# Reordering the opening, adj's squares and layer 1's last pair in a four-layer graph kernel bound by TensorE

## The chip, the cores and the metric

The kernel runs on one core of one Trainium2 chip. The metric is the device time of one execution in microseconds (us); smaller is better. Every experiment was timed on the same chip as the kernel before, in alternating rounds. All runs told of here were fast runs; their granted clock was 0.998 to 1.0 of full. A run takes about 970 us, so 1 us is 0.1%; differences under about 0.5 us are at the edge of what the timings can tell.

## The reference, cut to what matters

`x` has the shape 32 x 512 x 128 and `adj` 512 x 512, both float32. Each of four layers adds its output to `x`; each takes `h = relu(layernorm(x))` as input.

```python
# layer 0: masked softmax attention, one row of weights for all batches
m   = adj > 0
idx = jnp.cumsum(m.reshape(-1).astype(jnp.int32)) - 1
A   = softmax(where(m, e[0][idx], NEG), axis=1)
out = einsum('ij,bjg->big', A * I, h @ W[0]) + einsum('ij,bjg->big', A * (1 - I), h @ W[1]) + bias
# layer 1: Chebyshev hops with adj, then Theta and relu
x1 = einsum('bnf,nw->bwf', h, adj);  x2 = 2.0 * einsum('bnf,nw->bwf', x1, adj) - h
out = relu(concat(h, x1, x2, x1, x2) @ Theta + bias)
# layer 2: messages with adj * adj
features = relu(h @ psi_w + psi_b)
messages = einsum('nm,bnd->bmd', adj * adj, features)
out = relu(concat(messages, h) @ phi1_w + phi1_b) @ phi2_w + phi2_b
# layer 3: attention with tanh-clipped scores
A = exp(tanh(Q @ K.T / sqrt(128) / 8) * 8) * adj;  out = (A / A.sum(-1)) @ h @ v
```

## The kernel before: the parts that the change touches

The 32 batches are handled as 16 pairs (`NQ = 16`). The large products with adj use seven block products where eight would be plain (Strassen's scheme), so some operands are sums of blocks, made by VectorE (DVE) and GpSimd (POOL). Python generators interleave the work: each `yield` is a place where another stage's instructions may be put between. In the traces here each engine runs them in the order in which the program issues them (the products p_qk_t, p_later and p_qk, issued sooner, start at 8.6 to 9.8 us after the change and at 13.3 to 15.2 us before it). That order is what the change changes.

The opening finds, from `adj`, which value of `e` belongs to each entry, by products with 0/1 matrices; in the same time it normalises pair 0.

```python
    # adj > 0 and row counts rc, as adj lands; rch is their half-precision copy
    nc.vector.tensor_copy(rch, rc)
    # ... p_incl: cumulative counts, on TensorE
    keep_busy(7)                                   # dummy products p_idle
    early = [early_stats(q, q == 1) for q in range(2)]
    next(early[0])                                 # statistics of pair 0's first batch
    # ... known, incl, before
    go(normal[0], NT)                              # ScalarE normalises that batch
    for t in range(NT):                            # of_row on VectorE, p_row on TensorE
        # ...
    # ... p_known
    next(early[0])                                 # statistics of pair 0's second batch
    nc.tensor.transpose(p[:, blk(0)], qw, ident)   # layer 3's q and k
    nc.tensor.transpose(p[:, blk(1)], kw, ident)
    nc.scalar.copy(pgs[:, 0:2, :], pg[0])
    nc.vector.tensor_copy(pgs[:, 2:4, :], pg[1])
    # ... p_upto, which needs pgs
    nc.tensor.matmul(p_qk[:, :D], qkT[:, 0, :], qkT[:, 1, :], start=True, stop=True)
    for t in range(NT):                            # "mask products", p_later
        nc.tensor.matmul(scores[t], ident16, m[:, t, :], start=True, stop=False)
    go(normal[0])                                  # second batch of pair 0
    # ... p_hT: transposes of h; p_g: projections with W
```

adj transposed goes to memory by way of four VectorE transposes and four DMA writes; the same SyncE queue carries the feature-major copies hT of later pairs.

```python
    def turn_adj():
        for t in range(NT):
            nc.vector.transpose(ab[:, :, t, :], adj_s[:, t, :].rearrange(...))
            yield
        for b in range(NQR):
            nc.sync.dma_start(adjT_d[:, blk(b)]..., ab[b * QR : (b + 1) * QR]...)
    # in round 0 of layer 0:  step 3: go(squares, 2)   step 4: go(squares)
```

In layer 1 `first(C)` computes a hop, `weighed(C)` multiplies by Theta (32 products p_w), and `right_blocks` makes the sums that the second hop's products p_l need. Between them is a `yield`, which lets the next stage's products in; for the last pair, that is layer 2's.

```python
        weighed(A)
        first(C)
        yield
        def operands():
            weighed(C)
            return right_blocks(...)
        if r == 0:
            right2 = operands()
        yield
        if r > 0:
            right2 = operands()
        # ... the products p_l
        if C == NQ - 1:
            yield
            yield
            yield
        ln_stats(A)
        ln_stats(C)
```

## Time and profile before

| | kernel before |
|---|---|
| median of three runs | 971.31 us (971.03 to 971.39) |
| profiled span | 969.8 us |
| TensorE busy | 956.6 us, 99% |
| VectorE, ScalarE, GpSimd busy | 60%, 49%, 43% |
| mean granted TensorE clock | full |

TensorE (PE) leaves 13.2 us of its span unused, and the other engines are idle for about half of it. In such a kernel no other engine's total matters; only the single places do where PE stands and waits for one of them. The profile's lines for these places are in the prediction below. One caution on reading them: a matmul's end is modelled, so a PE that is slightly held up at every product looks busy. The distance between the starts of two products is the safer measure.

### The profile page before, as it was taken

Reading aid. Unit: us, or ns where it says so; the run is one execution under the profiler, and the core shown is the slowest. Engines: PE = TensorE matmul, PEld = TensorE weight load, DVE = VectorE, ACT = ScalarE, POOL = GpSimd, SP = SyncE. Lnnn points to the kernel's source line nnn. Section 1 sums busy time; section 2 is a strip of 40 time slices with the busy share of each in tenths; the row PEclk is TensorE's granted clock in tenths of the full one; section 3 lists DMA queues with packets and bytes.
Section 4 is the critical chain, followed back from the end, with each engine's and each line's share of the span. In section 5 each row is a group of like instructions: output and inputs, shape, how many; then the busy total and the mean of one; then the engine's idle time right before and its main releaser. Section 6 shows DMA issues by size and latency. Waiting matters only on the chain.

```text
span 969.8 us, 15164 instructions
## 1 busy us (share of the span) xinstructions
PE 956.6 (99%) x5473; PEld 780.9 (81%) x5473; DVE 584.6 (60%) x1332; ACT 471.1 (49%) x1055; POOL 421.1 (43%) x463
## 2 busy tenths in 40 slices
PE   8999999999999999999999999999999999999998
PEld 4889999898998989897887777777676777777776
DVE  7788986745546536646657756655654444454444
ACT  4864551452242233376628544455674445544553
POOL 4867997933417523512324443334042233223322
PEclk9999999999999999999999999999999999999999
DMA  9075643242341321343343332332131121121111
GB/s 247 21 195 163 175 109 99 74 123 66 95 139 33 82 70 40 109 109 88 72 125 108 110 87 66 87 88 73 57 100 56 49 73 54 57 74 45 55 33 44
DMA packets 83913, 86.04 MB, mean 89 GB/s; under 512 B 6784, under 2 KB 74624, under 8 KB 83840
## 3 DMA queue, kind: packets, MB, share of 16 engines
q1 hardware_dynamic: 83840, 85.09, 31.3%
q8 instruction: 43, 0.70, 0.3%
q14 instruction: 30, 0.25, 0.1%
HBM read 44.17 MB, written 40.89 MB: 88 GB/s over the span
## 4 chain that ended last, share of the span: by engine, by line
PE 90%; DVE 3%; POOL 2%; ACT 2%; DMA 1%; issue 1%; SPq 0%; DVEq 0%; POOLq 0%; ACTq 0%
PE p_av L1112 12%; PE p_score L1097 11%; PE p_l_c L382 7%; PE p_w L431 5%; PE p_l_d L382 5%; PE p_msgT_c L375 5%; PE p_x1T_c L375 4%; PE p_l_a L382 4%; PE p_hv L431 3%; PE p_l L431 3%; PE p_qkh L1084 3%; PE p_msgT_d L375 3%; PE p_feat L431 3%; PE p_phi L1067 3%; PE p_phi L1068 3%; PE p_msgT_a L375 3%
## 5 line engine op out<-in xcount | busy, mean ns | idle before, releaser
L243 ACT ACTIVATE h<-x,sh,rs 128x128 f32<-128x128 f32 x512 | 209.4, 484 | 65.6 <-PE p_x1T_d L375 21.6
L1102 POOL TENSOR_TENSOR ex<-ex,adjTx 128x512 f32<-128x512 f32 x62 | 80.4, 1297 | 208.2 <-ACT ex L1100 202.6
L1098 ACT ACTIVATE ex<-p_score 128x512 f32<-128x512 f32 x128 | 71.8, 587 | 122.9 <-issue 113.1
L1112 PEld LDWEIGHTS p_av<-qkh_hv,ex 128*128 128x128 f32 x1024 | 118.4, 191 | 8.4 <-issue 7.4
L1112 PE MATMUL p_av<-qkh_hv,ex 128*128 128x129 f32 x1024 | 119.9, 274 | 0.0
L1097 PE MATMUL p_score<-qkh_hv,hT 128*128 128x512 f32 x256 | 115.2, 593 | 0.0
L1102 DVE TENSOR_TENSOR ex<-ex,adjTx 128x512 f32<-128x512 f32 x66 | 46.1, 702 | 81.9 <-ACT ex L1100 81.9
L279 DVE STREAM_TRANSPOSE hb_hT<-h 128x512 f32<-128x512 f32 x120 | 81.9, 697 | 20.9 <-ACT h L243 19.2
L223 DVE BATCH_NORM_STATS2 bn<-x 128x6 f32<-128x256 f32 x248 | 89.8, 417 | 0.6
L1097 PEld LDWEIGHTS p_score<-qkh_hv,hT 128*128 128x128 f32 x256 | 46.2, 190 | 46.5 <-issue 44.7
L1100 ACT ACTIVATE ex<-ex 128x512 f32<-128x512 f32 x128 | 76.6, 630 | 1.8
L352 POOL TENSOR_TENSOR rt_feat<-feat,feat 128x256 f32<-128x256 f32 x16 | 11.6, 725 | 140.1 <-ACT feat L1051 140.1
L949 ACT COPY w<-p_w 128x512 f32<-128x512 f32 x32 | 18.2, 574 | 106.2 <-PE p_w L431 106.1
L352 POOL TENSOR_TENSOR rt_w<-w,rt_w 128x512 f32<-128x512 f32 x16 | 20.3, 1270 | 110.3 <-DVE rt_w L352 92.0
L431 PE MATMUL p_w<-th,x1T 128*128 128x128 f32 x256 | 49.5, 275 | 0.0
L431 PE MATMUL p_w<-th,hs 128*128 128x128 f32 x256 | 49.5, 275 | 0.0
L431 PEld LDWEIGHTS p_hv<-vw,hT 128*128 128x128 f32 x256 | 33.6, 192 | 15.3 <-issue 8.1
L1062 POOL TENSOR_TENSOR x<-x,phi2b 128x256 f32<-128x256 f32 x64 | 44.5, 726 | 0.0
L431 PEld LDWEIGHTS p_w<-th,hs 128*128 128x128 f32 x256 | 39.9, 192 | 0.7
L1117 DVE SCALAR_TENSOR_TENSOR x<-p_av,rsum,x 128x128 f32<-128x128 f32 x128 | 39.1, 347 | 1.9
L1051 ACT ACTIVATE feat<-feat 128x512 f32<-128x512 f32 x32 | 20.1, 629 | 40.9 <-DVE feat L1050 40.9
L700 POOL TENSOR_TENSOR hd<-hT,adiag 128x512 f32<-128x512 f32 x32 | 39.7, 1276 | 0.3 <-ACT adiag L827 0.3
(234 smaller groups left out, 2040.2 us busy)
## 6 DMA issues: line engine op xcount, KB each, us to landing
d_hT<-hb_hT SPq DMA_DIRECT2D x240, 128.0 KB
hT<-d_hT SPq DMA_DIRECT2D x60, 512.0 KB
x<-in_x_dram SPq DMA_DIRECT2D x32, 256.0 KB
out_dram<-x SPq DMA_DIRECT2D x31, 256.0 KB
adj_s<-in_adj_dram SPq DMA_DIRECT2D x4, 256.0 KB
adjT_d<-adj_squares SPq DMA_DIRECT2D x4, 256.0 KB
sq<-in_adj_dram SPq DMA_DIRECT2D x4, 256.0 KB
adjTx<-adjT_d SPq DMA_DIRECT2D x4, 256.0 KB
```

Of the source, the lines that this page charges most:

```text
L223: nc.vector.bn_stats(st[:, k].rearrange("p e s -> p (e s)"), xt[q][:, b, t : t + 2, :].rearrange("p t f -> p f t"))
L243: nc.scalar.activation(h[:, b, t, :], xt[q][:, b, t, :], AF.Relu, bias=shift[q][:, i : i + 1], scale=scale[q][:, i : i + 1])
L279: nc.vector.transpose(hb[:, :, b].rearrange("p j t r -> p t j r"), h[:, b].rearrange("p t (j c) -> p t j c", c=QR))
L375: nc.tensor.matmul(p[:, :H], b[:, k, :], a[:, k, :], start=(first and k == 0), stop=(k == 1), skip_group_check=True)
L382: nc.tensor.matmul(p[:, i * 2 * D : (i + 1) * 2 * D], a[:, k, blk(i)], b[:, k], start=(first and i == 0 and k == 0), stop=(k == 1), skip_g ...
L431: nc.tensor.matmul(p[:, blk(t)], hT(t), w, start=(i == 0), stop=(i == len(terms) - 1))
L1062: tc.keep_in_program_order(nc.gpsimd.tensor_add(xi, xi, spread(phi2b, 2)))
L1097: nc.tensor.matmul(ps, hT[:, t, b, :], qkh, start=True, stop=True)
L1098: nc.scalar.activation(ex[:, t, :], ps, AF.Tanh, scale=1.0 / (8.0 * math.sqrt(D)))
L1100: nc.scalar.activation(ex[:, t, :], ex[:, t, :], AF.Exp, scale=8.0)
L1102: eng.tensor_mul(split(ex[:, t, :]), split(ex[:, t, :]), crossed(adjTx[0][:, t, :]))
L1112: nc.tensor.matmul(po[:, i, : D + 1], ex[:, t, blk(i0 + i)], hv[:, t, :], start=(t == 0), stop=(t == NT - 1))
```

## The change

The intent is to close PE's holes by order alone: no product is added and none dropped but four dummies. It has four parts.

```diff
# 1. the opening
     for b in range(2):
         load_x(b)
+    qw = load_rows(q_w, "qw")[:, 0, :]          # before: behind the next two x loads
+    kw = load_rows(k_w, "kw")[:, 0, :]
 ...
             if whole and b == 0:
+                yield                           # pair 1's statistics in two parts
                 continue
 ...
-    keep_busy(7)
+    # one of known's two copies moves ahead of adj's as well
+    # q/k transposes and qkT's copy, mask products p_later, p_qk and qk's copy: here now
+    keep_busy(3)
     early = [early_stats(q, q == 1) for q in range(2)]
     next(early[0])
 ...
+    next(early[0])                              # pair 0's second statistics before of_row
 ...
-    go(normal[0], NT)
+    go(normal[0])                               # all eight normalisations before pgs
 ...                                             # row products p_row, p_known
-    next(early[0])
-    # (q/k transposes, p_qk, p_later, go(normal[0]) stood behind here)
+    next(early[1])

# 2. adj's squares: created before the first softmax, then one step at a time
     go(early_stats_2, 3)
+    next(squares)
 ...
                     next(left_of_att)
+                    next(squares)
                     go(ln3)
 ...
-                    go(squares, 2)              # step 3 of round 0
+                    go(squares)
 ...
-                    go(squares)                 # step 4 of round 0
 ...                                             # rounds 2 and up: one product later
-                if more and r > 1:
-                    go(projection(A + 2))       # step 1
-                if r == 1:
+                if more:
                     go(projection(A + 2))       # step 2

# 3. layer 1's last pair weighed sooner
-        if r == 0:
+        sooner = r == 0 or C == NQ - 1
+        if sooner:
             right2 = operands()
         yield
-        if r > 0:
+        if not sooner:
             right2 = operands()

# 4. its statistics in two rounds
-        if C == NQ - 1:
-            yield
-            yield
-            yield
-        ln_stats(A)
-        ln_stats(C)
+        if C < NQ - 1:
+            ln_stats(A)
+            ln_stats(C)
+
+    def layer1_stats():
+        ln_stats(NQ - 2)
+        yield
+        ln_stats(NQ - 1)
 ...
+    waiting[-NQ + 7].append(layer1_stats())
```

More of the change, by code (lines that the diff above doesn't have):

```diff
@@ L142 @@
         load_x(b)
-    qw = load_rows(q_w, "qw")[:, 0, :]
-    kw = load_rows(k_w, "kw")[:, 0, :]
     w0 = const.tile([P, 2, D], F32, name="w0")
@@ L183 @@
     nc.vector.memset(ones, 1.0)
+    known = prep.tile([P, NT, 2], F16, name="known")
+    nc.vector.tensor_copy(known[:, :, 1], rows)
     upto = prep.tile([P, NT, N], F16, name="upto")
@@ L515 @@
                              start=(s == 0), stop=(s == t))
-    keep_busy(7)
+    p = bank("p_qk_t")
+    nc.tensor.transpose(p[:, blk(0)], qw, ident)
+    nc.tensor.transpose(p[:, blk(1)], kw, ident)
+    qkT = prep.tile([P, 2, D], F32, name="qkT")
+    nc.scalar.copy(qkT, tiles(p)[:, :2, :])
+    scores = {}
+    for t in range(NT):
+        scores[t] = bank(f"p_later_{t}")
+        nc.tensor.matmul(scores[t], ident16, m[:, t, :], start=True, stop=False)
+    p_qk = bank("p_qk")
+    nc.tensor.matmul(p_qk[:, :D], qkT[:, 0, :], qkT[:, 1, :], start=True, stop=True)
+    qk = const.tile([P, D], F32, name="qk")
+    nc.scalar.copy(qk, p_qk[:, :D])
+    keep_busy(3)
     early = [early_stats(q, q == 1) for q in range(2)]
     next(early[0])
-    known = prep.tile([P, NT, 2], F16, name="known")
-    nc.vector.tensor_copy(known[:, :, 1], rows)
     incl = prep.tile([P, NT], F32, name="incl")
@@ L561 @@
                              start=(t == 0), stop=(t == NT - 1))
-    next(early[0])
-    p = bank("p_qk_t")
-    nc.tensor.transpose(p[:, blk(0)], qw, ident)
-    nc.tensor.transpose(p[:, blk(1)], kw, ident)
-    qkT = prep.tile([P, 2, D], F32, name="qkT")
+    next(early[1])
     pgs = prep.tile([P, NT, NE], F16, name="pgs")
@@ L570 @@
     nc.vector.tensor_copy(pgs[:, 2:4, :], pg[1])
-    nc.scalar.copy(qkT, tiles(p)[:, :2, :])
     row_of = prep.tile([P, NK], F32, name="row_of")
@@ L581 @@
                              start=(j == 0), stop=(j == NT - 1), skip_group_check=True)
-    p_qk = bank("p_qk")
-    nc.tensor.matmul(p_qk[:, :D], qkT[:, 0, :], qkT[:, 1, :], start=True, stop=True)
-    qk = const.tile([P, D], F32, name="qk")
-    nc.scalar.copy(qk, p_qk[:, :D])
-    scores = {}
-    for t in range(NT):
-        scores[t] = bank(f"p_later_{t}")
-        nc.tensor.matmul(scores[t], ident16, m[:, t, :], start=True, stop=False)
-    go(normal[0])
     copies = [nc.scalar.copy, (nc.scalar.copy, nc.vector.tensor_copy), nc.scalar.copy]
@@ L650 @@
     attT = square_tile("attT")
+    squares = turn_adj()
     early_stats_2 = stats_steps(2)
@@ L721 @@
     own, turning, hd, adiag = {}, {}, {}, []
-    squares = turn_adj()
     sums_ahead = late_sums()
```

## The prediction

> **What bounds the kernel now.** I read the page first, then the waits of TensorE (PE), the timeline of every engine over the first 75 us, and the queue of SyncE (SP), which issues the transfers.
>
> ```profile
> span 969.8 us, 15164 instructions
> PE 956.6 (99%) x5473; PEld 780.9 (81%) x5473; DVE 584.6 (60%) x1332; ACT 471.1 (49%) x1055; POOL 421.1 (43%) x463
> PE 90%; DVE 3%; POOL 2%; ACT 2%; DMA 1%; issue 1%; SPq 0%; DVEq 0%; POOLq 0%; ACTq 0%
> ```
>
> PE is the bound: it is idle for 969.8 - 956.6 = 13.2 us, and the chain that ended last is PE for nine tenths. No matrix work leaves the kernel except four dummy products, so the change can win only PE's holes. The waits of PE name them (line, releaser, total, count, longest):
>
> ```profile
> PE p_g L431 <- DMA hT<-d_hT: 2.1, 2, 1.2
> PE p_idle L496 <- DVE upto L186: 1.9, 1, 1.9
> PE p_incl L514 <- DVE rch L509: 1.0, 1, 1.0
> PE p_msgT_a L375 <- ACT feat L1051: 0.9, 1, 0.9
> PE p_msgT_c L375 <- POOL rt_feat L352: 0.7, 1, 0.7
> PE p_l_a L382 <- ACT w L949: 0.7, 1, 0.7
> PE p_msgT_c L375 <- DVE msgT L398: 0.6, 1, 0.6
> PE p_msgT_a L375 <- ACT msgT L396: 0.5, 1, 0.5
> ```
>
> The two waits on hT are at 60.93 and 70.87 us, the feat, msgT copy and rt_feat waits between 452 and 457 us, the one on DVE msgT at 515.43 us, the one on w at 390.00 us. Short stalls hide inside busy time, so I also compared start-to-start times with the usual one of each shape (0.112 us for a 128x128 f32 product, 0.216 us for 128x256 f32 or 128x512 f16). By that the hT holes are 1.33 and 1.12 us, the 452-457 ones 1.07 + 0.68 + 0.89 = 2.64 us, and the 515 one 0.78 us and 0.21 us right after it.
>
> The opening is the other place. PE's timeline (start, us, product):
>
> ```profile
> 10.51 2.75 PE L555 MATMUL p_row<-of_row,m 128*128 128x256 f16 x16 [0.33 <-DVE of_row L552]
> ...
> 13.72 1.37 PE L580 MATMUL p_upto<-upto,pgs 128*128 128x512 f16 x8
> 14.93 0.44 PE L583 MATMUL p_qk<-qkT 128*128 128x128 f32 x2
> 15.20 1.03 PE L589 MATMUL p_later<-m,ident 128*128 128x512 f16 x4
> 16.07 1.53 PE L261 MATMUL p_hT<-ident,h 128*128 128x128 f32 x8
> 17.74 2.05 PE L431 MATMUL p_g<-w,hT 128*128 128x128 f32 x16
> 19.63 0.59 PE L624 MATMUL p_later<-at_col,at_row 128*128 128x512 bf16 x2
> ```
>
> PE looks full, but the transposes p_hT take 17.74 - 16.07 = 1.67 us where eight cost 0.9: they wait for ScalarE (ACT), which normalises the second half of pair 0 only at 15.56 to 17.21, and p_qk and p_later stand before them. VectorE (DVE) is busy without a hole from 7.31 to 21.0 us, and ends the operands at_part of the value products at 20.23. SP's queue, last:
>
> ```profile
> 48.27 3.40 SPq L484 DMA_DIRECT2D adjT_d<-adj_squares  x4
> 51.85 3.48 SPq L286 DMA_DIRECT2D d_hT<-hb_hT  x4
> 57.45 0.34 SPq L288 DMA_DIRECT2D hT<-d_hT  x1
> ```
>
> The four writes of adj's squares are issued until 51.67, and the d_hT writes start only then, though DVE had finished hb_hT at 51.1. hT lands at 60.79, and PE's p_g starts at 60.93. This queue, not DVE's or ACT's share, makes the hole.
>
> **What the Trainium skill says.** "TensorE: Matmul & The Clock Gate", section "What's actually happening": PE runs at half clock until it has been busy for about 3.4 us, and again after an idle window of about that length. The trace agrees with the first half: the first eight p_idle products start 0.43 us apart, later ones 0.216. The longest hole is 1.9 us, so cutting the filler from seven to three is safe while holes stay under 2 us. Section "Back-to-back issue gap" of that page gives N/2.4 + 2.5 ns, 216 ns at N = 512; the four p_later products take 16.07 - 15.20 = 0.87 us, as it says. "DMA: Bandwidth & Descriptors", section "Anatomy of one DMA — SWDGE (gpsimd) path", fits a transfer as about 2.0 us plus bytes over 436 GB/s: 3.2 us for the 512 KB of hT; here, issued by SP, it took 60.79 - 57.45 = 3.34 us, so hT's two hops cannot get much shorter, they can only start sooner. "Perfetto Trace Analysis", its opening note, warns that matmul busy time is a bad metric of closeness to the limit, because matmuls are pipelined; the p_hT stretch above, busy on paper and stalled, agrees.
>
> **Part 1, the opening.** DVE now does pair 0's second statistics before of_row. One such block (two 128x256 statistics, two small operations) lasts from 8.17 to 9.12 = 0.95 us; known leaves the path (-0.08). So of_row ends 0.87 us later, 13.47 instead of 12.60, and p_row and p_known end about 14.17 instead of 13.30. Gone behind p_upto are p_qk (0.29) and p_later (0.87); gone before it are the two transposes of q and k (0.28); they move to PE's stretch between 8.66 and the row products, in place of four fillers (4 x 0.216 = 0.86 us). There they wait for q's and k's weights, which are now issued right behind the first two x blocks. The second of those lands at 9.06 by the queue's semaphores; two small transfers behind it came 0.25 us apart, so I estimate k's at 9.6 us. PE then runs transposes, p_later, p_qk and three fillers to about 11.55, with of_row's first part ready at about 11.3.
>
> ACT's order is the catch: it copies qkT and qk (until about 11.2), then does all eight normalisations of pair 0 (3.19 us a set of eight) to about 14.4, and only then pgs[0:2], until about 14.9. Before, that copy ended at 13.66. So p_upto starts at 14.95 and ends at 16.1; the transposes take 0.9 us straight away, hT's first copy ends at 17.15, p_g runs from 17.2 to 19.0. Before it started at 17.74: 0.54 us gained. DVE has the same work before at_part, so that still ends near 20.25; the last value product of row block 0 needs it and can end no sooner than 20.5, so 1.0 us is the ceiling of this part. I take 0.55 us.
>
> **Part 2, adj's squares one by one.** Four transposes of 0.65 us each move to earlier idle time of DVE (1.24 us before 32.78, 0.92 us before 39.19) and two stay at 41.5. adjT_d can be issued from about 42 us and landed, at 7.1 us from first issue to last landing as before, near 49, clear of d_hT. hb_hT of pair 4 is then bound by ACT's h, which ended at 50.27 (about 49.7 with part 1): d_hT issued from 50.55, 3.8 us to its landing as for the later set (69.33 to 73.15), so 54.4; hT 3.34 us later, 57.8. PE wants it at 60.93 - 1.33 - 0.55 = 59.05, so the hole of 1.33 us goes. SP's next x loads and d_hT follow hT's issue, which moves from 57.45 to 54.45; the chain from there to the second hT's landing was 70.83 - 57.45 = 13.4 us, so 67.85, and PE, 0.55 + 1.33 ahead, wants it at 70.87 - 1.12 - 1.88 = 67.87. That is level; I take 1.05 of the 1.12 us. The projections that go one product later in rounds 2 and up, where there is no hole now, are worth nothing but room: PE is now 3 us nearer to its transfers.
>
> **Part 3, layer 1's last pair.** Its 32 weighing products (32 x 0.112 = 3.6 us) now stand between p_feat of pair 0 and the first message products. feat and rt_feat were ready at 454.2 and 457.2; PE then asks for them at about 455.9 and from 457.6. The 2.64 us should go, less 0.25 for the DVE addition that waits for ACT's msgT copy behind the new w copies: 2.4 us. The wait at 390 us is another pair's, whose order does not change: it stays.
>
> **Part 4, its statistics.** Before 515 us DVE does three pairs' statistics in one round, twelve of 0.35 us. Now they are split, eight in each of two rounds: about 1.4 us less before the late one, against a hole of 0.78 + 0.21 us. I take 0.9.
>
> Sum: 0.55 + 1.33 + 1.05 + 2.4 + 0.9 = 6.2 us. All of it counts, since PE has no other hole of note after 75 us, and the end of the kernel is unchanged. 971.3 - 6.2 = 965.1.
>
> **Rivals.** (a) The opening gains nothing or loses: the 0.87 us of statistics on DVE's path and ACT's late pgs are real costs, and if k's weights land after 10.5 us, row products move too. Against it: p_upto may slip 1.2 us, and 1.16 (p_qk, p_later) plus 0.77 of stall leave behind it. If true, 966 to 967. (b) The earlier hT only uncovers the next wait: pair 5's chain is level within 0.02 us by my own sum, so PE may stand there again by up to a microsecond. 966. (c) In layer 2 the schedule turns over: the list of instructions shows many normalisations and transposes moved on ACT and DVE, and p_w's copies stand among them; a new wait for msgT or w of 1 us is easy. 966 to 967. (d) More than I take: the opening reaches its ceiling, 1.0, and all holes go: 964.3.
>
> **Range and chances.** The rivals lose more than (d) wins, so the range leans up: 965.2, from 963.8 to 967.8. A gain of 2% would be 19.4 us, more than all of PE's idle time of 13.2 us; a loss of 2% would need a hole that nothing here makes.
>
> **What would show it.** In the changed kernel: p_g's first product at about 17.2, and p_upto at about 14.95 waiting for ACT's pgs copy; SP's adjT_d issue at 42 and hT at about 54.4; no PE wait on hT near 60 us, and under 0.2 us near 68; no waits of PE between 448 and 456 us over 0.3 us; none near 508 to 515; the one on w (0.7 us) still there. It would be wrong if PE's idle time in the page falls by much less than 5 us, or if new waits appear on msgT or w.

## The result, and the profile after

| | before | after |
|---|---|---|
| median of six runs, same chip | 971.28 us (970.92 to 972.82) | 964.67 us (963.71 to 966.54) |
| profiled span | 969.8 us | 962.7 us |
| TensorE busy | 956.6 us | 953.7 us |
| TensorE idle (span less busy) | 13.2 us | 9.0 us |

The ratio is 0.9932, with a 95% interval from 0.9919 to 0.9945. Here and below, a ratio is the mean time of one kernel's fast runs over that of the other's of the same rounds, so it is not quite the ratio of the medians that I quote.

The head of the page of the kernel after, with its chain that ended last:

```profile
span 962.7 us, 15161 instructions
PE 953.7 (99%) x5469; PEld 780.9 (81%) x5469; DVE 585.3 (61%) x1332; ACT 470.1 (49%) x1055; POOL 421.7 (44%) x463
PE 96%; ACT 2%; DMA 1%; DVE 1%; SPq 0%; issue 0%; DVEq 0%; ACTq 0%
```

PE's share of the chain rises from 90% to 96%, with the work the same. Its busy time fell by 2.9 us though only four products of 0.216 us, 0.86 us, were dropped: the other 2 us were stalls that had passed for busy time. For the same reason PE's idle time fell by 4.2 us only, a little less than the 5 us that the prediction named as its sign. Its waits (line, releaser, total us, count, longest):

```profile
PE p_idle L500 <- DVE upto L189: 2.0, 1, 2.0
PE p_qk_t L522 <- DMA qw<-in_L_gnn_q_dram: 0.8, 1, 0.8
PE p_l_a L386 <- ACT w L949: 0.7, 1, 0.7
PE p_upto L590 <- ACT pgs L580: 0.6, 1, 0.6
PE p_incl L518 <- DVE rch L513: 0.4, 1, 0.4
PE p_g L435 <- ACT hT L268: 0.4, 2, 0.2
```

The waits on hT's transfer, on feat, rt_feat and msgT are gone. The wait on w is still there, and two are new: the q/k transposes wait for q's weights, and p_upto for ScalarE's copy pgs. Both were in the prediction. PE's timeline of the opening (start, us, product; in brackets the idle time before and its releaser) and ScalarE's beside it:

```profile
10.71 2.65 PE L571 MATMUL p_row<-of_row,m 128*128 128x256 f16 x16
...
14.13 1.26 PE L590 MATMUL p_upto<-upto,pgs 128*128 128x512 f16 x8 [0.59 <-ACT pgs L580]
15.23 1.04 PE L265 MATMUL p_hT<-ident,h 128*128 128x128 f32 x8
16.51 2.05 PE L435 MATMUL p_g<-w,hT 128*128 128x128 f32 x16 [0.24 <-ACT hT L268]
```

```profile
10.42 3.19 ACT L247 ACTIVATE h<-x,sh,rs 128x128 f32<-128x128 f32 x8
13.51 0.56 ACT L580 CAST pgs<-p_row 128x512 f16<-128x512 f32 x1
```

The transposes take 1.04 us where they took 1.53, and p_upto stands waiting for pgs, which ScalarE does only behind eight normalisations. SyncE's queue at the same place as in the prediction:

```profile
41.65 3.41 SPq L488 DMA_DIRECT2D adjT_d<-adj_squares  x4
50.08 1.75 SPq L290 DMA_DIRECT2D d_hT<-hb_hT  x4
53.98 0.34 SPq L292 DMA_DIRECT2D hT<-d_hT  x1
```

adjT_d is issued 6.6 us sooner and hT 3.5 us sooner (57.45 - 53.98); 0.8 us of each is that the whole run stands earlier, as told below. hT of pair 4 landed at 57.42 and PE asked for it at 58.41.

**Where the time went.** The adj loads land at a different time in every run: the last of their four blocks had landed at 7.29 us in the trace before and at 6.49 us in the trace after, and over the 14 traces the first cast that depends on them (`rch`) starts at 6.61 to 8.12 us, with no regard to the load order. 0.80 us of the 7.1 us between the two profiled spans is this chance. I therefore count positions from the start of that cast:

| from the start of rch, us | before | after | step before | step after | gain | predicted |
|---|---|---|---|---|---|---|
| first p_g of pair 0 | 9.70 | 9.27 | 9.70 | 9.27 | 0.43 | 0.55 |
| p_g of pair 4 | 52.89 | 51.17 | 43.19 | 41.90 | 1.29 | 1.33 |
| p_g of pair 5 | 62.83 | 60.01 | 9.94 | 8.84 | 1.10 | 1.05 |
| first p_feat (layer 2) | 442.50 | 439.73 | 379.67 | 379.72 | -0.05 | 0 |
| p_l of layer 1's last pair | 458.83 | 452.92 | 16.33 | 13.19 | 3.14 | 2.4 |
| first p_score (layer 3) | 677.42 | 670.82 | 218.59 | 217.90 | 0.69 | 0.9 |
| end | 961.75 | 955.44 | 284.33 | 284.62 | -0.29 | 0 |
| sum | | | | | 6.31 | 6.2 |

### The profile page after: what moved, and what is told of

It is laid out like the page before. It is cut to its first block, busy times and chain, and to the rows that moved or that the text cites.

```text
span 962.7 us, 15161 instructions
## 1 busy us (share of the span) xinstructions
PE 953.7 (99%) x5469; PEld 780.9 (81%) x5469; DVE 585.3 (61%) x1332; ACT 470.1 (49%) x1055; POOL 421.7 (44%) x463
## 4 chain that ended last, share of the span: by engine, by line
PE 96%; ACT 2%; DMA 1%; DVE 1%; SPq 0%; issue 0%; DVEq 0%; ACTq 0%
PE p_av L1116 12%; PE p_score L1101 11%; PE p_l_c L386 8%; PE p_w L435 6%; PE p_l_d L386 5%; PE p_msgT_c L379 5%; PE p_l_a L386 4%; PE p_x1T_c L379 4%; PE p_l L435 3%; PE p_feat L435 3%; PE p_hv L435 3%; PE p_msgT_d L379 3%; PE p_msgT_a L379 3%; PE p_phi L1071 3%; PE p_qkh L1088 3%; PE p_phi L1072 3%
```

## The experiments

All twelve runs gave correct results. "From rch" means a position counted as in the table above. Timed ranges are lowest to highest of fast runs; "before" is the kernel before in the same call.

### First call: each part undone

The kernel before had a median of 970.92 us (7 runs) here. By time alone only no_squares (interval of the ratio 0.9949 to 0.9979) and no_sooner (0.9952 to 0.9982) can be told from the kernel after (0.9919 to 0.9945); the intervals of no_opening (0.9924 to 0.9957) and no_split (0.9928 to 0.9957) overlap its own, so for those two the traces decide.

**no_opening**: the kernel after, with part 1 undone.

```diff
-    # q/k products and p_later ahead of the row products; second statistics before of_row;
-    # go(normal[0]) before pgs; keep_busy(3); q and k loaded early
+    # all as in the kernel before; parts 2 to 4 kept
```

> The changed kernel with the opening put back (statistics, q-k and mask products, order of the loads, seven fillers). Theory: in the profile of the changed kernel p_g started 1.23 us sooner, but 0.80 of that was the adj loads landing sooner in that one run (rch at 7.24 instead of 8.04 us), so the opening itself is worth 0.43 us; counted from rch, p_g should start 9.7 us later here as in the kernel before (9.27 in the changed one), and the time should be near 965.1. Rival 1: the opening is worth the whole 1.2 us, its order of loads brings adj sooner: rch stays near 8.0 here and the time is near 965.9. Rival 2: the 0.95 us of statistics on the vector engine's path ate the gain: no slower than the changed kernel, 964.7.

Measured: 965.11 us (965.05 to 965.20, 4 runs), ratio 0.9941. From rch, p_g starts at 9.68, as in the kernel before (9.70), so the 0.41 us at that place is the opening's. But PE's lead shrinks on the way: 0.28 us at the p_g of pair 5 (60.29 against 60.01), 0.18 at p_feat, 0.11 at the end (955.55 against 955.44). The second trace of the kernel after (after_again, below) has 60.34 at pair 5 and 955.55 at the end, so there nothing is left that these traces can tell. The lead at the first p_g itself is clear of that noise: p_g is at 9.08 to 9.42 in the eight traces with this opening, and at 9.68 and 9.70 in the two without it.

**no_squares**: the kernel after, with the transposes at their old places. The projections of rounds 2 and up keep their new place; they have a test of their own below.

```diff
-    next(squares)  # two single steps, then go(squares) in step 3
+    # step 3: go(squares, 2)   step 4: go(squares)
```

> The changed kernel with adj's four transposes back in their two pairs, the second after the statistics. Theory: both holes of PE on hT come back, 1.33 and 1.1 us, so 967.1; adjT_d is issued near 47 us and d_hT only behind it. Rival: with the opening sooner, the holes come back only in part or move to the next pair, 965 to 966; or the room that the projections gained absorbs the second hole, 965.8.

Measured: 967.42 us (966.88 to 967.93, 4 runs), ratio 0.9964, 2.75 us over the kernel after's 964.67. PE's wait and SyncE's queue in this run:

```profile
PE p_g L435 <- DMA hT<-d_hT: 2.6, 2, 1.4
```

```profile
47.72 3.39 SPq L488 DMA_DIRECT2D adjT_d<-adj_squares  x4
...
56.90 0.34 SPq L292 DMA_DIRECT2D hT<-d_hT  x1
```

Both holes are back with the late adjT_d issue, and the end from rch is 958.31, 2.87 us more than after. Part 2 carries more than a third of the gain.

**no_sooner**: part 3 undone.

```diff
-        sooner = r == 0 or C == NQ - 1
+        sooner = r == 0
```

> The changed kernel with layer 1's last pair weighed late again (its statistics still split). Theory: the three holes of PE between 448 and 456 us come back, 3.1 us counted from the first p_feat to p_l_a of the last pair, so 967.8. Rival: the holes came from the statistics or from the order the scheduler chose after them, then at most 1 us comes back, 965.7.

Measured: 967.83 us (966.97 to 968.00, 4 runs), ratio 0.9967. Its waits of PE show all three again:

```profile
PE p_msgT_a L379 <- ACT feat L1054: 0.9, 1, 0.9
...
PE p_msgT_c L379 <- POOL rt_feat L356: 0.7, 1, 0.7
...
PE p_msgT_a L379 <- ACT msgT L400: 0.5, 1, 0.5
```

The stretch from p_feat to layer 1's last p_l is 16.34 us, against 13.19 after and 16.33 before. The stretch from p_score to the end is 284.34, as in the kernel before, where every run with the weighing of the last pair alone moved has about 0.28 us more. In the kernel after, VectorE's last DRAIN instruction, in the barrier that closes the program, starts 2.47 us after its last sum into x has ended, against 2.10 us here. What holds it is not shown. With the weighing moved in every round (sooner_all and best, below) the stretch is 284.40 and 284.39.

**no_split**: part 4 undone.

```diff
-        if C < NQ - 1:
-            ln_stats(A); ln_stats(C)     # and layer1_stats
+        if C == NQ - 1:
+            yield; yield; yield
+        ln_stats(A); ln_stats(C)
```

> The changed kernel with the last pair's statistics again both in one round, three yields after its products. Theory: the PE hole of 0.78 + 0.21 us on the msgT addition near 508 us comes back; but splitting left stalls of some 0.15 us in each of two rounds, so the net is 0.4 to 0.6 us: 965.1 to 965.3. Rival: the hole is filled by the earlier weighing alone and nothing comes back: 964.7.

Measured: 965.23 us (964.62 to 966.06, 4 runs), ratio 0.9942. The wait of PE is there again:

```profile
PE p_msgT_c L379 <- DVE msgT L402: 0.6, 1, 0.6
```

From the last pair's p_l to the end the run takes 503.28 us, after 502.52: 0.76 us for the split.

### Second call: which pieces pay, and is there more

The kernel before had 971.58 us (9 runs). Two of the nine took 974.0 and 974.1 us; they count in the means, so this call's ratios flatter its kernels a little, all alike.

**products_only**: the kernel after without the sooner statistics and normalisations; the q/k and mask products stay ahead.

```diff
-    next(early[0])            # before of_row
+    # second next(early[0]) behind p_known, as before
-    go(normal[0])             # before pgs
+    go(normal[0], NT)
+    # go(normal[0]) behind p_upto, as before
```

> The changed kernel with the products of q-k and mask ahead, but pair 0's second statistics where they were (behind of_row). Counted from rch, the changed kernel's p_g starts at 9.27 us, with the whole opening undone at 9.68. Theory: the gain is the products' alone, the sooner statistics cost the vector engine's path what they save: of_row's end goes back from 5.47 to 4.57, p_upto starts near 5.7, the second half of pair 0 is normalised behind pgs until about 8.5, and p_g starts at 9.1 or earlier; the time stays within 0.3 us of the changed kernel (964.4 to 965.0). Rival: the statistics are what pays (the transposes wait for the second half): p_g at 9.7, as with the opening undone, and 965.1.

Measured: 965.09 us (964.55 to 965.57, 5 runs), ratio 0.9930. PE's timeline:

```profile
13.76 1.26 PE L588 MATMUL p_upto<-upto,pgs 128*128 128x512 f16 x8 [0.28 <-ACT pgs L578]
14.86 2.08 PE L264 MATMUL p_hT<-ident,h 128*128 128x128 f32 x8
17.07 2.05 PE L434 MATMUL p_g<-w,hT 128*128 128x128 f32 x16
```

With rch at 8.01, p_upto is at 5.75 and p_g at 9.06 from it, against 6.89 and 9.27 after. The transposes are slow again (2.08 us), waiting for normalisations, and yet p_g is 0.2 us sooner, since the row products did not wait for the second statistics; the traces with the whole opening have 9.08 to 9.42, so "not later" is as much as this shows. The opening's gain is the moved products'; the sooner statistics pay nothing that can be seen.

**qk_later**: ScalarE copies qk between the two halves of pair 0, so that its first normalisation need not wait for p_qk.

```diff
-    nc.scalar.copy(qk, p_qk[:, :D])
-    go(normal[0])
+    go(normal[0], NT)
+    nc.scalar.copy(qk, p_qk[:, :D])
+    go(normal[0])
```

> The changed kernel with one instruction of the scalar engine moved: the copy of qk goes behind the first half of pair 0's normalisation. Theory: the step I named the catch, the scalar engine's order, holds pgs up: pair 0's normalisation starts at 9.8 instead of 10.42 us, pgs is copied at 13.15 instead of 13.51 (from rch 5.9 instead of 6.27), p_upto and p_g start 0.36 us sooner (p_g 8.9 from rch); end 0.2 to 0.36 us sooner, so 964.4. Rival: the vector engine's at_part (ending 12.2 from rch) or the power of the second half on GpSimd holds the path: p_g under 0.15 us sooner, and the same time.

Measured: 964.87 us (964.70 to 965.39, 5 runs), ratio 0.9929. In this run the adj loads landed so early (rch at 6.61) that other things held of_row up: VectorE waited 0.10 us for x and then 0.44 us for p_incl, which started at 7.93 us, without idle time before it, behind PE's 16 dummies. So positions from rch don't compare. From of_row's end, p_upto comes at 1.10 us (after: 1.42) and p_g at 3.48 (after: 3.80): 0.32 us sooner, which confirms that ScalarE's order holds p_upto. But the p_g of pair 4 is 46.16 us from of_row's end, against 45.70 after: the lead is lost, and more. The list of waits shows a new one, and VectorE's and GpSimd's timelines the reason:

```profile
PE p_l_c L386 <- DVE u_l L788: 0.9, 1, 0.9
```

```profile
34.17 1.18 DVE L236 SCALAR_TENSOR_TENSOR sh<-bn,rs 128x8 f32<-128x8 f32 x1
...
38.74 0.96 DVE L236 SCALAR_TENSOR_TENSOR sh<-bn,rs 128x8 f32<-128x8 f32 x1
```

```profile
34.05 1.27 POOL L356 TENSOR_TENSOR rt_g<-g,rt_g 128x512 f32<-128x512 f32 x1
```

The operation sh on eight columns took 1.18 us and ended at 35.35 (34.17 + 1.18). The GpSimd operation had started before it, and ended at 35.32 (34.05 + 1.27). In the kernel after the same operation took 0.28:

```profile
34.14 0.28 DVE L236 SCALAR_TENSOR_TENSOR sh<-bn,rs 128x8 f32<-128x8 f32 x1
```

The Trainium skill, "SBUF — State Buffer", section "SBUF: two separate sides", says that VectorE and GpSimd share a pair of ports as an exclusive lock: a VectorE operation with two SBUF inputs, as this one, waits out the whole GpSimd operation that started first, if that one reads SBUF. The traces agree: of the 62 such sh operations in a run, 38 to 42 take over 0.3 us, and each of these ends 0.02 to 0.03 us after a GpSimd operation, before and after the change alike. None of the 20 to 24 shorter ones lies wholly inside a GpSimd operation. The one of 0.28 us had only met the end of one: it ended at 34.42 (34.14 + 0.28), and the GpSimd operation at 34.39 (33.11 + 1.28).

**sooner_all**: the weighing before the yield in every round.

```diff
-        sooner = r == 0 or C == NQ - 1
+        sooner = True
```

> The changed kernel with the second pair weighed sooner in every round of layer 1, not only in the first and the last. Theory: the one hole of PE left there (0.85 us before p_l_a near 385 us, on the copy of w behind eight normalisations) goes: 0.8 us less, 963.9. Rival: in the other rounds the order was already free of holes, and the moved products bring new waits on x1T or w: same or up to 1 us slower.

Measured: 962.93 us (962.59 to 963.08, 4 runs), ratio 0.9907, 1.7 us under the kernel after. From rch the end is 953.42, 2.02 us less. The remaining wait of p_l_a on w is gone from the list of waits. The gain is more than twice what I expected. From layer 1's first product to the first p_feat PE takes 1.53 us less (260.96 against 262.49; 262.44 in after_again): that hole of 0.85 us, and 0.7 us in stalls too short for the list of waits, of 0.16 to 0.17 us in six of the rounds. Another 0.22 us is the close, told of under no_sooner. The rest lies before layer 1, where two traces of the kernel after differ by as much. The 1.7 us in time is across calls; in the third call best, below, shows the same side by side.

**no_proj**: only the projections of rounds 2 to 6 moved back.

```diff
+                if more and r > 1:
+                    go(projection(A + 2))    # step 1
-                if more:
+                if r == 1:                   # step 2
```

> The changed kernel with the projections of rounds 2 to 6 one product sooner, as they were. Theory: no difference: in the changed kernel hT of pair 6 lands at 74.11 us and PE projects at 77.83, would at 76.10; pair 8 93.16, 97.06 and 95.3; so 964.7, no wait on hT. Rival: on transfers that land late in some runs, by 2 us and more, PE waits: holes of up to 0.5 us on hT in these rounds.

Measured: 964.79 us (964.36 to 964.87, 4 runs), ratio 0.9926; the end from rch is 955.22 (after: 955.44), and there is no wait on hT. This piece is worth nothing that these runs show.

### Third call: what stayed open

The kernel before had 970.87 us (9 runs).

**after_again**: the kernel after, unaltered.

> The changed kernel unaltered, as a control beside the next three on the same chip. In the traces so far the adj loads let rch start anywhere from 6.6 to 8.0 us, whatever the order of the loads, and this moves the whole run: expected 964.7, between 963.7 and 966.5; counted from rch, p_g at 9.2 to 9.3 and the end at 955.4.

Measured: 964.82 us (964.33 to 965.45, 5 runs), ratio 0.9936. From rch, p_g of pair 5 is at 60.34 with a wait on hT of 0.2 us before it, which the first trace did not have, and the end is 955.55. A second trace of one kernel thus differs by 0.1 us at the end and 0.3 us inside; differences of that size between the others tell nothing.

**opening_only**: the kernel before with part 1 alone.

```diff
+    # part 1 as in the kernel after; parts 2 to 4 as in the kernel before
```

> The kernel before with the opening of the changed kernel and nothing else. Theory: with adj's squares undisturbed, hT of pair 4 comes at a time set by SyncE's queue, and the 0.4 us that the opening wins at p_g is waited away there: PE's wait on hT grows from 2.1 to about 2.5 us, and the time stays as before, 970.9 to 971.6. Rival: the opening moves that queue too, and the whole 0.4 us stays: 970.5 and an unchanged wait of 2.1 us.

Measured: 970.62 us (970.23 to 971.19, 5 runs), ratio 0.9998, interval 0.9985 to 1.001: no difference that these runs can tell. I had thought that the wait on hT would grow by what PE gained. The trace says otherwise:

```profile
PE p_g L435 <- DMA hT<-d_hT: 2.0, 2, 1.1
```

The wait did not grow (2.1 before), so hT's transfers came sooner along with PE in this run; in no_squares, which has the same order on every engine up to there, it was 2.6. Two traces don't settle what the queue does. From rch this run ends at 961.18, 0.57 us sooner than the kernel before, so its one trace, unlike the timing and unlike no_opening, does show the lead kept to the end.

**qk_later_halves**: qk_later, with the long GpSimd operations near 34 and 38 us cut in two, so that the lock is held for half as long.

```diff
-            engs[i].tensor_sub(t[i], p, q)
+            for k in range(2):               # "g_0" only
+                engs[i].tensor_sub(t[i][:, k], p[:, k], q[:, k])
 ...
-            nc.gpsimd.tensor_mul(split(s), src, split(scale))
+            for k in (slice(0, 2), slice(2, 4)):   # hd of pair 0 and 1 only
+                nc.gpsimd.tensor_mul(split(s)[:, k], src[:, k], split(scale)[:, k])
```

> qk_later with GpSimd's eight operations of round 0 on 128x512 (rt_g, hd) cut into two of half the size each, nothing else. In qk_later p_upto and p_g did start 0.32 us sooner after of_row, but two tiny operations of the vector engine (sh from bn and rs, 128x8) took 1.18 and 0.96 us instead of 0.28 and 0.21, both ending 0.02 us after a GpSimd operation ended, and PE then waited 0.86 us for u_l behind them. Theory: that operation cannot run while a GpSimd operation does, and waits it out: with halves of about 0.7 us none of the two takes over 0.75 us, they end just after a half ends, and PE's wait on u_l falls from 0.86 to under 0.4 us; time 964.4 or less, against 964.9. Rival: the length comes from something else (PE, memory): the two stay near 1.0 us.

Measured: 965.66 us (964.49 to 967.56, 5 runs), ratio 0.9947. The two sh operations took 0.27 and 0.49 us in place of 1.18 and 0.96, and PE's wait on u_l is gone, which fits the lock as its cause. It isn't proof, since adj landed 0.8 us later in this run and moved the engines against each other: the first sh ended 0.03 us after a half that it met near its end. The time is no better for it: the end from rch is 955.52, and other small waits came up (0.7 us on ScalarE's hT copies, 0.2 on hT's transfer). In these runs a quicker opening did not make the kernel quicker.

**best**: products_only and sooner_all together.

```diff
-    # sooner statistics and normalisations of pair 0
-        sooner = r == 0 or C == NQ - 1
+        sooner = True
```

> The changed kernel with the second pair weighed sooner in all rounds of layer 1 (worth 2.0 us counted from rch) and with pair 0's second statistics back behind of_row (worth 0.1 to 0.2 us there). Theory: the two add: end at 953.3 from rch, 962.7 us, 2 us under the changed kernel of the same call, no PE wait on w. Rival: as with qk_later, the shifted opening meets GpSimd's operations badly and loses up to 0.9 us again: 963.5.

Measured: 962.87 us (961.86 to 963.90, 4 runs), ratio 0.9917, interval 0.9904 to 0.9931. It beats both kernels, by 8.0 us the kernel before of its call and by some 1.9 us after_again. It can't be told apart from sooner_all. The end from rch, expected at 953.3, is 954.36; rch was early here too (6.83), and VectorE waited 0.31 us for x and 0.46 us for p_incl, so this neither confirms nor refutes that the two gains add. Its list of PE's waits, whole as the view gives it:

```profile
PE p_idle L499 <- DVE upto L189: 2.0, 1, 2.0
PE p_upto L588 <- ACT pgs L578: 0.3, 1, 0.3
PE p_g L434 <- ACT hT L267: 0.3, 1, 0.3
PE p_x1T_c L378 <- DVE x1T L401: 0.2, 1, 0.2
```

## Why the prediction was right

The predicted 965.2 us and the range from 963.8 to 967.8 hold the measured 964.67, and the sum of the steps is 6.2 us predicted and 6.31 in the traces. That agreement is closer than the steps deserve, and in part luck: part 3 was 0.74 us too small, and the other rows of the table together 0.66 us too large.

- **Part 1, the opening: mechanism right, value at the end less.** The chain was as worked out: of_row ends 0.90 us later from rch (predicted 0.87), and p_upto waits for ScalarE's pgs copy behind eight normalisations and starts 6.89 us from rch (predicted 14.95 - 8.04 = 6.91). p_g is 0.43 us sooner, not 0.55: from p_upto's start to p_g's, transposes and copy took 2.38 us (14.13 to 16.51) where I had allowed 2.25 (14.95 to 17.2). What failed is the sentence that all of it counts: no_opening loses 0.41 us at p_g and 0.11 at the end, opening_only gains nothing that the timing can tell, and qk_later wins another 0.32 us at p_g and nothing in time. The median of no_opening is 0.4 us over the kernel after's. In the one trace of opening_only the end from rch is 0.57 us sooner. So the opening is worth between nothing and some 0.6 us, and these runs can't say more. Rival (a), that the opening gains nothing, is nearly true at the end of the kernel, by another way than the one that I gave.
- **Part 2, adj's squares: right.** 1.29 and 1.10 us against 1.33 and 1.05, and no_squares brings both holes back. The projections' move is worth nothing, as said. Rival (b), a wait on hT near 68 us, came up in some runs, at 0 to 0.3 us, where I had said up to a microsecond.
- **Part 3, layer 1's last pair: mechanism right, the term too small.** 3.14 us against 2.4. The three holes I had measured were 2.64 us, and all went: after the change every product in the stretch starts at its usual distance. The other 0.50 us were smaller stalls that I had not counted: 0.12 in p_feat, 0.2 in two p_msgT_a and 0.18 in p_msgT_c, by the sums of the distances from start to start of each kind (16.33 us before, 13.19 after). The 0.25 us that I took off for the addition behind the msgT copy did not come. Against it stand 0.29 us at the close of the program, which I had not foreseen, so part 3's net worth is about 2.85 us; no_sooner's end from rch, 958.12, is 2.68 us more than after.
- **Part 4, its statistics: right, a little less.** 0.69 us in the two traces and 0.76 by no_split, against 0.9. Stalls of about 0.13 us at p_msgT_c stay in the later rounds. Rival (c), a layer 2 schedule that turns over into new waits, didn't come.
- **The wait on w stayed**, as predicted (0.7 us). sooner_all shows that it and its smaller like in every round were there to be had by the same edit.

What stays open: what the opening is worth in time; what holds VectorE's last DRAIN back by 0.28 us at the close; and why the adj loads' landing moves by 1.5 us from run to run, which is as large as a whole part of this change.

## What to carry to other kernels

When one engine is 99% busy, add up its holes, by start-to-start distances and not by the list of waits alone: the stalls too short for the list were 0.5 us in one stretch and 0.7 us in layer 1's rounds. Ask of each hole which queue or engine's order made it, since here four DMA writes, issued late ahead of others in one queue, cost 2.4 us. And a lead won at the start is worth only what the later waits leave of it: move all the rounds that have the same pattern, rather than the one where the hole is seen.

## What the Trainium skill lacked or had wrong

- "SBUF — State Buffer" has the lock between VectorE and GpSimd right, but gives no cost for tiny operations: here one of 128x8 elements took 1.18 us where the same one took 0.28 in another run, and 38 to 42 of 62 in each run took over 0.3 us; the median of the others is 0.17 us.
- "DMA: Bandwidth & Descriptors" gives fixed costs, and no page has how far the landing of a program's first loads varies from run to run: the last of the four 256 KB blocks of adj landed at 5.85 to 7.37 us over 14 traces.
- The fit of that page for a 512 KB transfer, 3.2 us, stands for transfers issued by GpSimd; issued by SyncE it took 3.34 us before (60.79 - 57.45) and 3.44 after (57.42 - 53.98), so it serves there too, slightly low.
- "TensorE: Matmul & The Clock Gate", section "Back-to-back issue gap", gives for a stream of weight loads and products about 131 ns a product at N = 512, and calls its formula (216 ns) that of a lone one. Here the formula holds in the stream: every product has its weight load (5473 of each before), and the four p_later products start 0.215 to 0.216 us apart.
- That page's re-throttling was not put to the test: the longest hole after the warm-up was 1.4 us (no_squares), and the granted clock stayed full with it; no run had one near the idle window of about 3.4 us that the page gives.
